# Four graph layers on one core: products of zeros at the start, two pairs fetched into idle places, later weights through GpSimd's queue

## The chip, the cores and the metric

The kernel runs on one core of a Trainium2 chip. The metric is the device time of one execution in microseconds. The kernel before was run three times: 521.82 us median, 519.45 to 524.5.

## The reference, cut to what matters

Four graph layers run one after the other on 3327 nodes of 64 features and one dense 3327 x 3327 adjacency matrix of floats. Each layer adds its result to its input and normalises each row.

```python
x = _layernorm(x + _L0_gnn_ref(x, adj, L0_gnn_W), axis=-1)
x = _layernorm(x + _L1_gnn_ref(x, adj, L1_gnn_weight, L1_gnn_bias), axis=-1)
x = _layernorm(x + _L2_gnn_ref(x, adj, L2_gnn_W, L2_gnn_b), axis=-1)
x = _layernorm(x + _L3_gnn_ref(x, adj, L3_gnn_weight, L3_gnn_bias), axis=-1)
```

The change is in layer 0, and in what layer 0 computes ahead for layer 3:

```python
# layer 0
neigh = jnp.matmul(adj, features)
deg = jnp.sum(adj, axis=1, keepdims=True) + 1.0
neigh = neigh / deg
data = jnp.concatenate([features, neigh], axis=-1)
return jnp.matmul(data, W.T)
# layer 3: only the last 100 neighbours of a node count
mask = (adj != 0).astype(support.dtype)
rank = jnp.cumsum(mask, axis=1)
```

## The kernel before, in words

**Tiling.** The nodes are padded to 26 blocks of 128. The adjacency matrix is stored transposed and read in four column chunks (CH = 832 nodes) by 13 pairs of row blocks: one pair is a tile of 128 x 2 x 832 floats, 832 KB. Every layer reads all 52 pairs again. In layer 0 the chunks go in the order 0, 3, 1, 2 (`ORDER`), and in each chunk the pairs go from jp = 12 down to jp = 0. `load_adj` (L307) issues a pair on SP's queue into the pool `adjp` of four buffers; a fifth load waits until the first buffer is free.

**Own features.** `load_xt` (L733) fetches the transposed features into `ut`, the first half of the tile `uw`: first the columns of the last blocks, and after three pairs the rest. `own_features` multiplies some blocks by the turned weights `w0r` (L686), into a bank of PSUM. ScalarE copies one half of the result to `x0w` (L692), the stationary operand of the aggregation, and VectorE copies the other to `xr` (L693). It is called at the pairs named in `heads`: jp 12, 11, 9, 6 and 2. The weights `w0` come on ScalarE's queue and are turned on VectorE (L177 to L188).

**One pair.** `aggregate_pair` (L482) adds the pair's product with `x0w` to the chunk's accumulator. For three of the four chunks the pair is also ranked for layer 3. VectorE makes a mask of nonzeros (L508). TensorE counts along it with triangular matrices (L554) in two banks, of the three that `own_features` also uses. ScalarE writes the ranks (L564), and VectorE carries the last row of the count into the mask of the next pair (L540). `count` is let behind: up to `L0_SPILL` = 6 masks are open at the end of the first chunk, and the second chunk, which isn't ranked, works them off.

**Order on each engine.** A scheduler places the instructions; `issue_after` gives it orderings. Each engine then works its queue in order. On VectorE the first three masks stand ahead of the first two `xr` copies, and the first count's bank is read by the first of those copies.

**Later weights.** At jp = 7 of the first chunk `load_weights` (L201 to L207) issues seven small loads on SP's queue, for layers 1 to 3. At jp = 2 `later_weights` turns them on VectorE (`turn` makes `w1h`) and sends two products through TensorE (L706, L707); the results go to `w1r`, `wl1` and `wl2` by copies of VectorE and ScalarE and memsets of GpSimd.

**The idle places.** `wt`, the second half of `uw`, is first written by `transposes0` in the second chunk. It holds two pairs. `half_of` gives one half of such a tile the shape of a pair; before, it stands further down, where layers 1 and 2 use it.

Of the kernel before, what the change touches and what calls it, by code (L numbers as in the profile page):

```python
# [21 lines left out]
BF = mybir.dt.bfloat16  # L22
# [10 lines left out]
P = 128  # L33
NB = 26
NP = NB * P
D = 64
CH = 832
HC = CH // 2
NCH = NP // CH

ORDER = (0, 3, 1, 2)
# [38 lines left out]

L0_SPILL = 6
L0_LAG = 3


L1_ENGINES = "GVGGGV"
# [42 lines left out]
def four_gnn_layers_kernel(  # L128
# [14 lines left out]
    nc = tc.nc  # L143
# [6 lines left out]
    setup = setup_stack.enter_context(tc.tile_pool(name="setup", bufs=1))  # L150
# [10 lines left out]
        out=basis, in_=basis, compare_op=ALU.not_equal, fill=55.0 / 56, base=0,  # L161
# [5 lines left out]
    def issue_after(ins, other):  # L167
        tc.add_manual_dep(
            ins.ins, other.ins.name,
            mybir.DependencyInfo(mybir.DependencyClass.NoSync, mybir.DependencyReason.DATA),  # L170
            reason="order",
        )
# [20 lines left out]
    w1s = setup.tile([D, D], FP, name="w1s")  # L193
    w2s = const.tile([D, 2, D], FP, name="w2s")
    w3s = const.tile([P, D], FP, name="w3s")
    b2s = const.tile([1, D], FP, name="b2s")
    bias = {name: const.tile([P, 1, D], FP, name=f"bias_{name}") for name in ("b1", "b3")}

    def load_weights():

        nc.sync.dma_start(out=w1s, in_=w1)  # L201
        nc.sync.dma_start(out=w2s, in_=w2.rearrange("(t k) f -> k t f", t=2))
        for h in range(2):
            nc.sync.dma_start(out=w3s[h * D : (h + 1) * D, :], in_=w3)
        nc.sync.dma_start(out=b2s, in_=b2.partition_broadcast(1))
        nc.sync.dma_start(out=bias["b1"][:, 0, :], in_=b1.partition_broadcast(P))
        nc.sync.dma_start(out=bias["b3"][:, 0, :], in_=b3.partition_broadcast(P))  # L207


    sign = const.tile([P, 1], FP, name="sign")  # L210
# [13 lines left out]
        out=tri, in_=tri, compare_op=ALU.is_gt, fill=0.0, base=0,  # L224
# [3 lines left out]
        out=tri, in_=tri, compare_op=ALU.not_equal, fill=float(MAX_NEIGH), base=0,  # L228
# [9 lines left out]
    for t, value in ((minus_last, -1.0), (last_bias, 200.0)):  # L238
        nc.gpsimd.memset(t, 0.0)
        nc.gpsimd.affine_select(  # L240
            out=t, in_=t, compare_op=ALU.not_equal, fill=value, base=1 - P,
# [11 lines left out]
        out=real, in_=real, compare_op=ALU.is_ge, fill=0.0, base=N - 1,  # L253
# [30 lines left out]
    ut, wt = uw[:, 0, :], uw[:, 1, :]  # L284
# [9 lines left out]
    last_rank = uw.rearrange("p t n -> p (t n)").bitcast(U8)[:, 0 : NB * CH]  # L294
    last_rank = last_rank.rearrange("p (b i) -> p b i", b=NB)


    def load_adj(c, jp, t=None):


        if isinstance(t, list):
            for k in range(2):
                nc.sync.dma_start(out=t[k], in_=adjt[c, 2 * jp + k])
            return t
        if t is None:
            t = adjp.tile([P, 2, CH], FP, name="adj", tag="adj")
        nc.sync.dma_start(out=t, in_=adjt[c, 2 * jp : 2 * jp + 2].rearrange("b p i -> p b i"))  # L307
        return t
# [236 lines left out]
    def count(masked, places, left=0, behind=None):  # L545

        issued = None
        while len(masked) > left:
            ranks, jp, mask, _ = masked.pop(0)
            counts = [places.zero(), places.one()]  # L550
            for k, lhsT, of in ((0, tri, 0), (1, tri, 1), (0, minus, 1)):
                for h in range(2):
                    for rows in (slice(0, D), slice(D, P)):
                        issued = nc.tensor.matmul(  # L554
                            counts[k][rows, h, 0:HC], lhsT=lhsT[:, rows],
                            rhs=mask[:, of, bass.ts(h, HC)],
                            start=lhsT is tri, stop=(k == 1 or lhsT is minus),
                        )
                        if behind is not None:
                            issue_after(issued, behind)  # L560
            ranks.after = counts[0]
            carry(masked)
            for k in (1, 0):
                ranks.made = nc.scalar.activation(  # L564
                    halves(ranks.rank[:, 2 * jp + k, :]), counts[k][:, :, 0:HC], AF.Relu,
                    bias=last_bias,
                )
        return issued
# [105 lines left out]
    with ExitStack() as l0s:  # L674
        banks = Banks(l0s, "l0psum")
        l0 = l0s.enter_context(tc.tile_pool(name="l0", bufs=1))
        mp = l0s.enter_context(tc.tile_pool(name="l0m", bufs=L0_SPILL + 3))
        places = Places(banks)
        x0w = l0.tile([P, NB, D], FP, name="x0w")
        nc.gpsimd.memset(x0w[:, :, 0:1], 1.0)  # L680

# [50 lines left out]
        def load_xt(cols):  # L732
            nc.sync.dma_start(out=ut[0:D, cols], in_=xt[:, cols])  # L733
# [2 lines left out]
        heads = {12: (24, 26), 11: (20, 24), 9: (13, 20), 6: (6, 13), 2: (0, 6)}  # L736
        first = GROUPS[3][0] * P
        load_xt(slice(first, NP))
        loaded = {jp: load_adj(ORDER[0], jp) for jp in (12, 11, 10)}
        load_xt(slice(0, first))  # L740
        masked, issued, counted, side = [], None, None, None
        for n, c in enumerate(ORDER):
# [4 lines left out]
            for jp in reversed(range(NB // 2)):  # L747
                owned = None
                if n == 0 and jp in heads:
                    owned = own_features(*heads[jp], issued if jp < 11 else None)  # L750
                a2 = loaded.pop(jp) if n == 0 and jp in loaded else load_adj(c, jp)
                issued = aggregate_pair(
                    acc, x0w, a2, jp, jp == NB // 2 - 1, jp == 0, counted or owned
                )
                if ranks:
                    mask = ranks.mask(jp, a2)
                    if n == 0:
                        issue_after(mask, turned)
                left = (L0_SPILL - jp // 2 if ranks else jp // 2) if n < 2 else L0_LAG
                counted = count(masked, places, left, issued)  # L760


                if side is not None and jp < NB // 2 - 1:
                    on_array = jp == NB // 2 - 2
                    if not step(side, (counted or issued) if on_array else mask if ranks else None):
                        side = None
                        transposes0(ORDER[n - 1], places.free(), counted or issued, True)
                        if n == NCH - 1:

                            nc.scalar.activation(nothing, wt[:, GROUPS[ORDER[n - 1]][0] * P].unsqueeze(1), AF.Tanh)  # L770
                if n == 0 and jp == 7:
                    load_weights()
                if n == 0 and jp == 2:
                    later_weights(mask)
# [412 lines left out]

    def half_of(t, k):
        return t[:, bass.ts(k, 2 * CH)].rearrange("p (b i) -> p b i", b=2)

    def load_ahead2(more):

        def load(k, t):
            return load_adj(ORDER2[0], PAIRS[k], t)

        loaded = [load(k, half_of(*t)) for k, t in enumerate(((ut, 0), (wt, 0), (wt, 1)))]
        yield loaded
        places = [[more(2 * i + k) for k in range(2)] for i in range(4)]
        loaded += [load(3 + k, t) for k, t in enumerate((*places, half_of(ut, 1)))]
        yield
        loaded.append(load(8, half_of(ut, 0)))
# [383 lines left out]
    with tc.If(some_near == 0) as cmp:  # L1590
        with ExitStack() as arm:
            banks = Banks(arm, "psum_far")
            layers_2_and_3(banks, *layer1_far(banks))
    with cmp.Else():
        done = layer1_near()
        with ExitStack() as arm:
            banks = Banks(arm, "psum_near")
# [47 lines left out]
```

## Time and profile before

| | |
|---|---|
| time, three runs | 521.82 us median, 519.45 to 524.5 |
| the profiled execution | 521.32 us, span 519.6 us |
| TensorE (PE) busy | 472.2 us, 91% |
| VectorE (DVE) busy | 392.6 us, 76% |
| ScalarE (ACT) busy | 341.2 us, 66% |
| GpSimd (POOL) busy | 205.9 us, 40% |
| moved by DMA | 132.49 MB, mean 255 GB/s |
| mean granted clock of TensorE | 0.986 |

Busy time is a share of the whole span; the stages differ. A line of the timeline gives start, duration, engine, source line, operation, tiles and count, and in brackets the idle time of the engine before it and what ended it. A line of the waits gives engine, tile and line, who was waited for, and then the total, the number and the longest of the waits. A line of the stretches gives the window, its length, busy time and instructions of PE, PE's weight loads, DVE, ACT and POOL, then PE's granted clock, the DMA share and GB/s. SPq is SP's DMA queue.

### The profile page before, as it was taken

How to read it: one execution, taken by the hardware profiler on the slowest of the kernel's cores; microseconds unless marked ns; L12 is line 12 of the kernel's file. 1: busy time of each engine (PE TensorE's matmuls, PEld its weight loads, DVE VectorE, ACT ScalarE, POOL GpSimd, SP SyncE). 2: the span in 40 equal slices, each digit the busy share in tenths (PEclk: the TensorE clock that was granted, in tenths of full speed). 3: DMA queues.
4: the chain of work that ended last, by engine and by line, in shares of the span. 5: the costliest groups of instructions: out<-in, count | busy, mean ns of one | idle time of the engine just before them, and what ended most of it. 6: DMA issues, size and time to landing. Idle time of an engine off the chain costs nothing. (4 is left out here: it accounts for less than half of the span.)

```text
span 519.6 us, 7871 instructions
## 1 busy us (share of the span) xinstructions
PE 472.2 (91%) x2888; PEld 241.7 (47%) x2888; DVE 392.6 (76%) x717; ACT 341.2 (66%) x422; POOL 205.9 (40%) x171
## 2 busy tenths in 40 slices
PE   5999999999967999999999999999999999899892
PEld 3554343454433333443353344354465555467781
DVE  3566428989767987789879977988789487737894
ACT  1345544776877899968987796820278845579862
POOL 2000200203017778966896785700412053410650
PEclk9999999999998999999999999999999999999995
DMA  8899999989529678767776777579969889960002
GB/s 271 280 387 322 390 376 368 356 289 328 199 69 308 241 264 280 245 198 256 252 245 202 236 259 261 197 275 401 316 195 360 305 289 345 316 240 2 0 2 71
DMA packets 46289, 132.49 MB, mean 255 GB/s; under 512 B 7046, under 2 KB 7150, under 8 KB 46178
## 3 DMA queue, kind: packets, MB, share of 16 engines
q1 hardware_dynamic: 45714, 131.36, 72.4%
q0 software_dynamic: 384, 0.52, 0.4%
q8 instruction: 24, 0.39, 0.3%
q14 instruction: 23, 0.19, 0.1%
q10 hardware_dynamic: 144, 0.03, 0.0%
HBM read 130.88 MB, written 0.85 MB: 254 GB/s over the span
## 5 line engine op out<-in xcount | busy, mean ns | idle before, releaser
L878 POOL TENSOR_TENSOR s<-s,p 128x832 f32<-128x832 f32 x67 | 130.2, 1957 | 43.5 <-ACT s L877 27.9
L863 DVE SCALAR_TENSOR_TENSOR p<-two,adj 128x832 f32<-128x832 f32 x100 | 101.1, 1018 | 19.7 <-issue 12.9
L564 ACT ACTIVATE rank<-two,last_bias 128x832 uint8<-128x832 f32 x78 | 71.7, 953 | 46.4 <-PE two L554 24.5
L852 PE MATMUL two<-uw 64*128 64x416 f32 x416 | 89.7, 545 | 13.1 <-DVE s L871 6.0
L482 PE MATMUL one<-adj,x0w 128*64 128x416 f32 x416 | 83.0, 524 | 3.8 <-DMA adj<-in_adjt_dram 2.4
L883 PE MATMUL one<-s,xu 128*64 128x416 f32 x416 | 85.2, 524 | 0.0
L540 DVE SCALAR_TENSOR_TENSOR mask<-two,minus_last,mask 32x832 bf16<-32x832 f32 x48 | 52.5, 1093 | 32.8 <-PE two L554 28.7
L876 ACT ACTIVATE s<-two 128x832 f32<-128x832 f32 x67 | 57.7, 861 | 28.8 <-DVE p L863 25.6
L852 PEld LDWEIGHTS two<-uw 64*128 64x128 f32 x416 | 38.2, 189 | 64.6 <-PE one L883 20.7
L508 DVE TENSOR_SCALAR mask<-adj 128x1664 bf16<-128x1664 f32 x48 | 51.3, 1070 | 14.0 <-DMA adj<-in_adjt_dram 13.5
L877 ACT ACTIVATE s<-s 128x832 f32<-128x832 f32 x67 | 60.1, 897 | 1.9
L554 PE MATMUL two<-mask,tri 128*64 128x416 bf16 x416 | 53.3, 345 | 8.5 <-DVE mask L540 5.4
L482 PE MATMUL one<-adj,xr 128*64 128x416 f32 x264 | 53.7, 517 | 2.4 <-DMA adj<-in_adjt_dram 2.4
L883 PEld LDWEIGHTS one<-s,xu 128*64 128x64 f32 x416 | 25.8, 136 | 47.5 <-issue 46.7
L482 PEld LDWEIGHTS one<-adj,x0w 128*64 128x64 f32 x416 | 29.0, 138 | 36.8 <-issue 23.6
L554 PEld LDWEIGHTS <-tri 128*64 128x64 bf16 x416 | 26.2, 110 | 40.9 <-issue 24.3
L1375 ACT ACTIVATE bits<-rank 128x832 fp32r<-128x832 uint8 (+1 forms) x42 | 38.8, 987 | 6.9 <-PE two L1430 5.1
L1371 POOL TENSOR_SCALAR bits<-exponents 128x832 fp32r<-128x832 bf16 (+1 forms) x21 | 26.0, 1255 | 40.5 <-DVE exponents L1353 20.4
L871 DVE SCALAR_TENSOR_TENSOR s<-two,p 128x832 f32<-128x832 f32 x37 | 37.5, 1015 | 1.4 <-ACT two L868 1.3
L868 ACT ACTIVATE two<-two 128x832 f32<-128x832 f32 x37 | 31.3, 847 | 5.4 <-DVE p L863 4.6
L1430 PE MATMUL two<-bits,parts 128*128 128x416 f32 x144 | 30.9, 360 | 2.5 <-POOL bits L1371 2.4
L482 PEld LDWEIGHTS one<-adj,xr 128*64 128x64 f32 x264 | 21.0, 136 | 23.2 <-issue 16.5
(290 smaller groups left out, 542.4 us busy)
## 6 DMA issues: line engine op xcount, KB each, us to landing
adj<-in_adjt_dram SPq DMA_DIRECT2D x135, 832.0 KB, 5.5
uw<-in_adjt_dram SPq DMA_DIRECT2D x7, 832.0 KB, 6.2
a<-in_adjt_dram SPq DMA_DIRECT2D x8, 416.0 KB, 6.5
sums<-in_adjt_dram SPq DMA_DIRECT2D x2, 832.0 KB, 7.4
p<-in_adjt_dram SPq DMA_DIRECT2D x4, 416.0 KB, 4.9
s<-in_adjt_dram SPq DMA_DIRECT2D x4, 416.0 KB, 6.5
uw<-in_xt_dram SPq DMA_DIRECT2D x1, 640.0 KB
out_dram<-o SPq DMA_DIRECT2D x2, 192.0 KB, 2.3
```

The lines of the kernel that those rows point to most:

```text
L482: issued = nc.tensor.matmul(acc[h * D : (h + 1) * D, 0:HC], lhsT=x[:, 2 * jp + k, 0:D], rhs=a[:, bass.ts(h, HC)], start=(first and k == 1) ...
L508: issued = nc.vector.tensor_scalar(mask, a2, 0.0, None, op0=ALU.not_equal)
L540: ranks.carried = nc.vector.scalar_tensor_tensor(halves(last), ranks.after[P - 32 : P, :, 0:HC], minus_last[P - 32 : P, :], halves(last), ...
L554: issued = nc.tensor.matmul(counts[k][rows, h, 0:HC], lhsT=lhsT[:, rows], rhs=mask[:, of, bass.ts(h, HC)], start=lhsT is tri, stop=(k == 1 ...
L564: ranks.made = nc.scalar.activation(halves(ranks.rank[:, 2 * jp + k, :]), counts[k][:, :, 0:HC], AF.Relu, bias=last_bias,)
L852: issued = nc.tensor.matmul(v[:, h, 0:HC], lhsT=wt[rows, bass.ts(jb, P)], rhs=ut[rows, bass.ds(c * CH + h * HC, HC)], start=True, stop=True,)
L863: issued = nc.vector.scalar_tensor_tensor(halves(p), v, 0.25 - 0.5 * FD, halves(a), op0=ALU.add, op1=ALU.mult)
L876: nc.scalar.activation(halves(s), v, AF.Square, bias=FB - 0.5, scale=-2.0)
L877: nc.scalar.activation(s, s, AF.Copy, bias=FG)
L878: nc.gpsimd.tensor_mul(s, s, p)
L883: issued = nc.tensor.matmul(acc[h * D : (h + 1) * D, 0:HC], lhsT=xu[:, jb, 0:D], rhs=s[:, bass.ts(h, HC)], start=first, stop=last,)
L1375: issued = nc.scalar.activation(t, src[:, b, :], AF.Exp, bias=-127.0 * LN2, scale=LN2)
```

## The change

A tile of zeros is cleared by VectorE, and thirteen bf16 products of it (`L0_IDLE`) go through TensorE into a bank that the counts use later, ahead of the first own features. The first two pairs of the first chunk (jp 12 and 11) go into the two halves of `wt`; the third goes into the pool, whose four buffers then take jp 10, 9, 8 and 7. The seven loads of `load_weights` move from SP's queue to GpSimd's, where they stand behind the memset of `x0w`. `half_of` is defined further up.

```diff
+L0_IDLE = 13
...
     def load_weights():
-        nc.sync.dma_start(out=w1s, in_=w1)
-        nc.sync.dma_start(out=w2s, in_=w2.rearrange("(t k) f -> k t f", t=2))
+        nc.gpsimd.dma_start(out=w1s, in_=w1)
+        nc.gpsimd.dma_start(out=w2s, in_=w2.rearrange("(t k) f -> k t f", t=2))
         for h in range(2):
-            nc.sync.dma_start(out=w3s[h * D : (h + 1) * D, :], in_=w3)
-        nc.sync.dma_start(out=b2s, in_=b2.partition_broadcast(1))
-        nc.sync.dma_start(out=bias["b1"][:, 0, :], in_=b1.partition_broadcast(P))
-        nc.sync.dma_start(out=bias["b3"][:, 0, :], in_=b3.partition_broadcast(P))
+            nc.gpsimd.dma_start(out=w3s[h * D : (h + 1) * D, :], in_=w3)
+        nc.gpsimd.dma_start(out=b2s, in_=b2.partition_broadcast(1))
+        nc.gpsimd.dma_start(out=bias["b1"][:, 0, :], in_=b1.partition_broadcast(P))
+        nc.gpsimd.dma_start(out=bias["b3"][:, 0, :], in_=b3.partition_broadcast(P))
...
+    def half_of(t, k):
+        return t[:, bass.ts(k, 2 * CH)].rearrange("p (b i) -> p b i", b=2)
...
         places = Places(banks)
+        zeros = setup.tile([P, HC], BF, name="zeros")
+        nc.vector.memset(zeros, 0.0)
+        idle = banks.pair(1)
+        for _ in range(L0_IDLE):
+            nc.tensor.matmul(
+                idle[:, 0, 0:HC], lhsT=zeros[:, 0:P], rhs=zeros, start=True, stop=True
+            )
...
         load_xt(slice(first, NP))
-        loaded = {jp: load_adj(ORDER[0], jp) for jp in (12, 11, 10)}
+        loaded = {
+            jp: load_adj(ORDER[0], jp, half_of(wt, 12 - jp) if jp > 10 else None)
+            for jp in (12, 11, 10)
+        }
         load_xt(slice(0, first))
```

The scheduler's order changes with it in a few places of the first chunk. On TensorE the two products of `later_weights` stand right behind the last own features and ahead of pair 2's aggregation, where before they stood behind the count that follows that aggregation. On VectorE the turning of the later weights moves ahead of the last `xr` copy, and the mask of pair 6 and that of pair 2 move ahead of a carry. On ScalarE the two copies into `wl1` and `wl2` move ahead of and between two rank writes. Behind the first steps of the second chunk the order on every engine is as before.

## The prediction

> **What bounds the kernel now.** I read the page's slices first (where the transfers pause), then busy time by stretches, then the waits, then the timeline of the first 45 us, because every edit acts there. Pairs of adjacency blocks are called by their jp: 12 comes first, 0 last.
>
> The stretches (length, busy us and instructions of each engine, clock, DMA share, GB/s):
>
> ```profile
> 20.00:22.00 2.00, 1.16 (x9) 0.53 (x10) 1.62 (x3) 0.80 (x2) 0.00 (x0) 1.00 0.24 45
> 24.00:41.00 17.00, 16.44 (x126) 9.09 (x120) 11.94 (x26) 7.35 (x9) 0.00 (x0) 1.00 1.00 372
> 41.00:48.00 7.00, 7.00 (x48) 3.20 (x48) 3.85 (x8) 4.60 (x8) 0.78 (x5) 1.00 0.86 261
> 48.00:60.00 12.00, 11.47 (x84) 4.86 (x80) 7.44 (x25) 6.80 (x9) 3.16 (x4) 1.00 1.02 391
> 60.00:76.00 16.00, 14.42 (x100) 6.78 (x98) 3.21 (x3) 8.98 (x11) 0.29 (x1) 1.00 1.02 388
> ```
>
> TensorE is full until 48 us, while the transfers have a hole at 20 to 22 us (45 GB/s) and are thin at 41 to 48 us (261 GB/s). From 48 to 76 us, the second chunk, the transfers are full (391 GB/s) and TensorE has holes. So the first chunk is paced by TensorE and the second by the transfers. The waits say the same:
>
> ```profile
> PE two L554 <- DVE xr L693: 0.7, 1, 0.7
> ...
> SPq L307 <- PE one L482: 77.3, 46, 4.3
> ```
>
> Between 12 and 45 us no TensorE matmul waits for a pair of the adjacency; SP's queue waits for TensorE to release one of four buffers. The start itself:
>
> ```profile
> 8.64 3.04 PE L482 MATMUL one<-adj,x0w 128*64 128x416 f32 x8
> ...
> 11.09 1.03 DVE L508 TENSOR_SCALAR mask<-adj 128x1664 bf16<-128x1664 f32 x1 [1.60 <-DMA adj<-in_adjt_dram]
> 12.03 0.61 DVE L693 COPY xr<-two 128x126 f32<-128x126 f32 x2
> 12.37 1.60 PE L554 MATMUL two<-mask,tri 128*64 128x416 bf16 x8 [0.68 <-DVE xr L693]
> ...
> 16.26 0.47 SPq L201 DMA_DIRECT2D w1s<-in_w_dram  x1
> ...
> 20.91 19.13 SPq L307 DMA_DIRECT2D adj<-in_adjt_dram  x9
> ...
> 24.75 1.57 PE L482 MATMUL one<-adj,x0w 128*64 128x416 f32 x8
> ```
>
> The same eight products take 3.04 us at 8.64 and 1.57 us at 24.75: TensorE starts at half clock. The clock record of the trace begins at full speed at 14.03 us. But the chain at the start isn't TensorE's. The first count (L554, 12.37) wants a bank that the xr copy (L693) reads; that copy stands on VectorE behind the mask of pair 10, the third pair, which landed at 11.09. That order on VectorE (three masks, then the copies) is the same in the changed program.
>
> **The change part by part.** The sum starts from the profiled execution, 521.32 us (span 519.6, 1.7 around it). The median of the three runs is 521.82, their spread 519.45 to 524.5.
>
> *Thirteen products of zeros.* VectorE clears the tile ahead of its first work at 4.44 us, by a memset like GpSimd's 0.2 us ones. A bf16 product of 416 columns takes 0.35 us at half clock (the L554 pairs at 12.37), so 13 x 0.35 = 4.55 us, from about 1.1 to 5.7 us. First operands come at 5.79: on the path 0 to +0.2 us, and I take 0, since the next wait (12.37) covers it. If the clock is then full, twelve feature products (2.93 us) and eight aggregations (3.04 us) take 1.5 each and end near 8.9 instead of 11.68. The gain is a longer wait for the same xr copy: 0.
>
> *What the clock does in that wait.* TensorE would be idle from 8.9 to 12.4, 3.5 us. What idleness did later in this trace:
>
> ```profile
> 157.39:160.80 3.41, 1.21 (x6) 0.30 (x4) 3.41 (x5) 3.23 (x4) 1.67 (x4) 1.00 1.06 377
> 160.80:164.21 3.41, 3.32 (x10) 1.90 (x12) 1.40 (x3) 2.58 (x4) 3.41 (x3) 0.50 1.04 268
> ...
> 505.55:508.96 3.41, 1.83 (x15) 1.55 (x13) 2.26 (x8) 1.08 (x2) 0.00 (x0) 1.00 0.48 118
> ```
>
> The record changes at 14.03, 160.80, 164.21 and 508.96, all whole multiples of 3.413 us apart. A stretch of that length with TensorE busy 1.21 us (36%) was followed by half clock, and so was one at 1.83 us (54%); 2.01 and 2.12 us (59 and 62%) were not. However the grid lies, a hole of 3.5 us leaves one stretch under 50%, so by the nearest rows the clock falls again and rises only after a well-filled stretch, somewhere from 14.3 to 18.6 us, against 14.03 now. Ends: if it stays full, the first count takes 1.05 instead of 1.85 us and the rank, the carry (L540) and the second count (17.02) follow 0.7 us earlier: -0.7. If it is half until 18.6, the aggregations of pairs 11 and 10 (2.8 us at full clock) take up to 2.3 us more: +2.3. For half clock until 15.7, the middle of the grid, it is +0.9. I weigh falling twice as heavy as staying: +0.4.
>
> [...]
>
> *Pairs 12 and 11 into idle places.* Now the fifth and sixth pairs (8 and 7) are issued at 11.72 and 15.84, each on a release by TensorE. In the changed program they go out at once behind pair 9. SP then issues pair 6 near 17, when pair 10 is released, and no longer at 20.91. From pair 5 on every issue waits for the same TensorE release as before (22.51 now, behind the aggregation that ended at 22.25). Nothing on TensorE waited for pairs 9 to 0, so their earlier landing hides nothing: 0. If the transfers were the bound, closing the hole would bring 2.0 x (391 - 45)/391 = 1.8 us; that is the far end.
>
> *Weights on GpSimd's queue.* Seven issues leave SP, where they held it from 16.26 to 20.1; that is the lateness of pair 6 above, counted already. GpSimd issues loads at 0.51 to 0.73 us each (155 to 158 us), so from about 4 to 8 us; three memsets queued behind them (L715 to L717) are wanted only in layer 1. Their 577 packets of 256 B at 18 ns are 0.68 us of the 16 engines. They now fall into full transfers, partly ahead of pair 10, whose landing sets 12.37: 0 to +0.7, taken +0.2.
>
> *What the scheduler moves.* The two products of later_weights (L706, L707) now stand right behind the last own features and ahead of pair 2. There TensorE waits for ScalarE today:
>
> ```profile
> 38.02 1.62 PE L482 MATMUL one<-adj,x0w 128*64 128x416 f32 x8 [0.56 <-ACT x0w L692]
> ...
> 40.62 0.33 PE L706 MATMUL two<-w1h,basis 64*64 64x64 f32 x2
> ```
>
> They cost 0.47 us at 40.62 (to 41.09) and would fill that wait: -0.45. But they need w1h, which VectorE makes 1.04 us after starting (38.46 to 39.50), now behind the mask of pair 2 and a carry (1.09). If mask 2 starts at 34.4, w1h is there at 37.5 and TensorE, free at 37.45, loses nothing. Mask 2 started at 35.69; if it does again, w1h comes at 38.8 and everything behind L706 is 1.2 us late. Ends -0.45 and +1.2; taken -0.45, since pair 2's transfer has less queued ahead of it. The carry for pair 0 moves behind the mask of pair 0 on VectorE, to about 42.7, still ahead of its count (43.98 now): 0.
>
> Sum: 0 + 0.4 + 0 + 0.2 - 0.45 = +0.15, so 521.5 us. A shift at the end of the first chunk goes on whole: the second is a closed loop of transfers that begins with releases by TensorE, and what follows has TensorE or VectorE over 85% busy (76 to 100 us: 22.98 and 20.55 of 24).
>
> **The rivals.**
>
> *Transfers set the first 48 us.* For it: both thin stretches, and eight TensorE waits for pairs, 6.5 us, from 45 to 80 us. Then the hole gives 1.8 us, the thin stretch 7 x (391 - 261)/391 = 2.3, the clock 0.7 and the moved products 0.45: 5.25, so 516.1 us. Against it: no TensorE wait for a pair between 12 and 45 us, and four buffers as before from pair 5 on, so the thin stretch stays.
>
> *The clock falls in the new hole and stays down until 18.6 us.* It decides from a rise later than 14.5 us on. Price +2.3 in place of +0.4: 523.4 us, slower than before. For it: the 36% and 54% stretches. Against: it needs an unlucky grid.
>
> *L706 waits for w1h at the head of TensorE's queue.* It decides if mask 2 starts later than 34.4 us; price 1.65 against the sum: 523.2. For it: mask 2 at 35.69 now. Against: pair 6 is issued 3 to 4 us earlier.
>
> *The zeros don't do what they are for:* the clock rises at 14 us as now. Then the 0.4 goes: 521.1.
>
> **How the numbers follow.** Forecast 0.50, transfers 0.12, clock down 0.18, w1h 0.12, idle zeros 0.08. The forecast is 521.5, no change. About 1% (5.2 us) is what a measurement of this kernel can tell from no change. The term bounds give 520.2 (-0.7 - 0.45) to 525.7 (0.2 + 2.3 + 0.7 + 1.2). The spread of the runs and part of the transfer case widen the lower side, and the top is cut where all bad ends would have to meet: 517.3 to 524.6. Faster by over 1% (under 516.6) is half the transfer case and a little scatter: 0.07. Slower by over 1% (over 527.0) needs two bad ends together: 0.05. Within: 0.88.
>
> **What would show it.** Right: L554's first count still at 12.3 to 12.8 behind the xr copy; L482's first eight in under 2.2 us; a half-clock stretch or 0.70 us steps of L482 again after 12 us; pair 6 issued near 17; the last aggregation of the first chunk ending within 2 us of 45; waits for pairs in the second chunk as now. Wrong: the second count (17.02) or the second chunk starting over 2.5 us earlier, the thin stretch at 41 to 48 us gone, or any difference made behind 80 us.

## The result, and the profile after

The changed kernel takes 527.33 us (median of 6 runs, 525.88 to 530.19) against 521.5 us for the kernel before in the same session (6 runs, 519.45 to 524.5). The ratio is 1.0119, 95% interval 1.0086 to 1.0152: 5.8 us slower, above the upper end of the forecast's range. The ratios, here and below, come from fast runs alone and are not quotients of two medians, from which they can differ by up to half a per cent. The profiled execution took 527.99 us, its span is 526.3 us (519.6 before), the mean granted clock 0.976 (0.986 before). Most lines of the changed kernel stand 6 to 13 further down: L482 is now L488, L508 L514, L540 L546, L554 L560, L564 L570, L692 and L693 are L705 and L706, L706 and L707 are L719 and L720, L597 is L603. The products of zeros are L689. In the other kernels the numbers shift again by a few lines.

The same stretches as before the change, with the hole of the transfers, which moved, in a stretch of its own (length, busy us and instructions of PE, PEld, DVE, ACT and POOL, clock, DMA share, GB/s):

```profile
20.00:22.00 2.00, 1.39 (x13) 1.20 (x11) 1.80 (x2) 1.47 (x3) 0.00 (x0) 1.00 1.03 388
22.00:24.00 2.00, 1.77 (x10) 0.77 (x12) 1.55 (x2) 0.17 (x1) 0.00 (x0) 1.00 0.30 112
24.00:41.00 17.00, 14.83 (x110) 8.23 (x106) 9.90 (x19) 6.16 (x8) 0.00 (x0) 0.97 0.90 312
41.00:48.00 7.00, 6.67 (x30) 3.02 (x32) 4.58 (x15) 1.82 (x5) 1.69 (x5) 0.58 0.47 152
48.00:60.00 12.00, 12.00 (x92) 5.81 (x90) 4.33 (x13) 7.39 (x9) 0.99 (x1) 1.00 0.97 339
```

The hole at 20 us is filled (45 GB/s before, 388 now) and another stands at 22 us (112 GB/s, and 83 from 24 to 26 us). The new thing is in the third and fourth rows. From 24 to 41 us TensorE did 110 instructions where it did 126, and from 41 to 48 us the clock is 0.58 where it was 1.00. By 48 us the second chunk, which used to begin at 45.03, has not begun. The timeline puts its first transposes 5.7 us later, of the 6.7 us by which the span is longer (before, then after):

```profile
49.09 0.58 PE L597 MATMUL one<-ident,sums 64*128 64x64 f32 x6
```

```profile
54.76 0.58 PE L603 MATMUL one<-ident,sums 64*128 64x64 f32 x6
```

The waits from 12 to 48 us (total, times, longest):

```profile
DVE mask L514 <- DMA adj<-in_adjt_dram: 8.2, 5, 2.5
...
ACT rank L570 <- DVE mask L546: 6.4, 4, 3.6
...
PE two L560 <- DVE xr L706: 4.0, 1, 4.0
...
PE two L719 <- DVE turn_m L186: 2.5, 1, 2.5
```

TensorE has two long waits: 4.0 us for the xr copy, which was 0.7 us before, and 2.5 us at the head of its queue, in L719, the first later-weight product, where before no wait in that place exceeded 0.6 us. The timeline at the first:

```profile
1.21 4.69 PE L689 MATMUL two<-zeros 128*128 128x416 bf16 x13 [1.21 <-DVE zeros L686]
5.89 1.60 PE L699 MATMUL two<-w0r,uw 64*128 64x128 f32 x12
7.43 1.62 PE L488 MATMUL one<-uw,x0w 128*64 128x416 f32 x8
...
13.01 1.60 PE L560 MATMUL two<-mask,tri 128*64 128x416 bf16 x8 [3.96 <-DVE xr L706]
```

The zeros do what they are for: the twelve own features take 1.60 us (2.93 before) and the first eight aggregations 1.62 (3.04). They end at 9.04 us, and TensorE then idles until 13.01, because the xr copy still stands on VectorE behind the mask of pair 10:

```profile
11.73 1.03 DVE L514 TENSOR_SCALAR mask<-adj 128x1664 bf16<-128x1664 f32 x1 [2.17 <-DMA adj<-in_adjt_dram]
```

That mask began at 11.09 before; it is 0.64 us later. At the second wait, before and after:

```profile
34.56 1.09 DVE L540 SCALAR_TENSOR_TENSOR mask<-two,minus_last,mask 32x832 bf16<-32x832 f32 x1 [0.18 <-PE two L554]
35.69 1.03 DVE L508 TENSOR_SCALAR mask<-adj 128x1664 bf16<-128x1664 f32 x1
...
37.49 0.47 ACT L692 COPY x0w<-two 128x378 f32<-128x378 f32 x1 [0.84 <-PE two L686]
```

```profile
37.23 1.60 PE L699 MATMUL two<-w0r,uw 64*128 64x128 f32 x12
...
37.95 1.03 DVE L514 TENSOR_SCALAR mask<-adj 128x1664 bf16<-128x1664 f32 x1 [2.45 <-DMA adj<-in_adjt_dram]
39.01 1.09 DVE L546 SCALAR_TENSOR_TENSOR mask<-two,minus_last,mask 32x832 bf16<-32x832 f32 x1
...
40.14 0.95 ACT L570 ACTIVATE rank<-two,last_bias 128x832 uint8<-128x832 f32 x1 [3.60 <-DVE mask L546]
...
40.94 0.24 DVE L187 TENSOR_SCALAR w1h<-w1s,turn_m 64x63 f32<-64x63 f32 x1
40.99 0.47 ACT L705 COPY x0w<-two 128x378 f32<-128x378 f32 x1
...
41.33 0.44 PE L719 MATMUL two<-w1h,basis 64*64 64x64 f32 x2 [2.50 <-DVE turn_m L186]
```

VectorE waits 2.45 us for pair 2 to land, then makes its mask, then the carry (L546; before, the carry came first, at 34.56 us), then what leads to w1h. On ScalarE the rank waits 3.60 us for that carry, and the x0w copy for pair 2 stands behind the rank. So two things that TensorE needs next, w1h and x0w, are both late by a wait for a transfer that neither of them reads.

Pair 2 is late for two reasons. SP issues it when TensorE releases its buffer, and that came 1.4 us later than before (29.66 us before, then 31.04), about as much as TensorE had lost at the start (the second count came at 18.39 us, before at 17.02). And the transfer itself took 6.9 us from issue to landing where it had taken 5.8; over the 19 profiles it took 4.7 to 6.9 us.

```profile
29.66 0.37 SPq L307 DMA_DIRECT2D adj<-in_adjt_dram  x1
```

```profile
31.04 0.37 SPq L313 DMA_DIRECT2D adj<-in_adjt_dram  x1
```

Both waits cost twice. These are the stretches around them of the grid on which the clock's record changes (at 5.92, 12.75, 16.16, 40.06 and 46.88 us in this profile, all whole multiples of 3.413 us apart):

```profile
9.34:12.75 3.41, 0.00 (x0) 0.00 (x0) 1.24 (x3) 0.00 (x0) 0.44 (x3) 1.00 1.12 290
12.75:16.16 3.41, 3.16 (x16) 1.96 (x17) 0.53 (x3) 1.46 (x2) 0.00 (x0) 0.50 0.94 288
...
36.64:40.06 3.41, 2.19 (x16) 1.41 (x12) 2.07 (x2) 0.00 (x0) 0.00 (x0) 1.00 1.02 367
40.06:43.47 3.41, 2.14 (x8) 1.02 (x10) 3.35 (x21) 1.36 (x3) 0.02 (x1) 0.50 0.76 303
43.47:46.88 3.41, 3.41 (x18) 1.53 (x16) 1.31 (x3) 0.45 (x2) 1.53 (x4) 0.50 0.21 21
```

After each wait TensorE runs at half clock: 12.75 to 16.16, and 40.06 to 46.88 us, where the aggregation of pair 2 takes 3.04 us in place of 1.62.

### The profile page after: what moved, and what is told of

The parts are those of the page before. It is cut to its first block, busy times and chain, and to the rows that moved or that the text cites. A ratio compares the mean times of both kernels' runs of the same rounds, so it can differ in the third digit from the quotient of the medians.

```text
span 526.3 us, 7899 instructions
## 1 busy us (share of the span) xinstructions
PE 477.7 (91%) x2901; PEld 243.3 (46%) x2901; DVE 392.6 (75%) x718; ACT 341.1 (65%) x422; POOL 212.5 (40%) x178
## 5 line engine op out<-in xcount | busy, mean ns | idle before, releaser
L570 ACT ACTIVATE rank<-two,last_bias 128x832 uint8<-128x832 f32 x78 | 71.7, 953 | 52.1 <-PE two L560 26.0
L488 PE MATMUL one<-adj,x0w 128*64 128x416 f32 x400 | 79.6, 524 | 3.1 <-DMA adj<-in_adjt_dram 2.2
L546 DVE SCALAR_TENSOR_TENSOR mask<-two,minus_last,mask 32x832 bf16<-32x832 f32 x48 | 52.5, 1093 | 33.9 <-PE two L560 29.6
L560 PE MATMUL two<-mask,tri 128*64 128x416 bf16 x416 | 53.9, 350 | 11.8 <-DVE mask L546 5.4
L514 DVE TENSOR_SCALAR mask<-adj 128x1664 bf16<-128x1664 f32 x46 | 48.6, 1057 | 18.9 <-DMA adj<-in_adjt_dram 18.4
L488 PE MATMUL one<-adj,xr 128*64 128x416 f32 x264 | 54.0, 517 | 2.2 <-DMA adj<-in_adjt_dram 2.2
L560 PEld LDWEIGHTS <-tri 128*64 128x64 bf16 x416 | 26.3, 111 | 44.2 <-issue 27.9
L488 PEld LDWEIGHTS one<-adj,x0w 128*64 128x64 f32 x400 | 28.1, 139 | 35.0 <-issue 23.6
L488 PEld LDWEIGHTS one<-adj,xr 128*64 128x64 f32 x264 | 20.9, 136 | 23.3 <-issue 16.1
```

Source lines behind the costliest of these rows:

```text
L488: issued = nc.tensor.matmul(acc[h * D : (h + 1) * D, 0:HC], lhsT=x[:, 2 * jp + k, 0:D], rhs=a[:, bass.ts(h, HC)], start=(first and k == 1) ...
L514: issued = nc.vector.tensor_scalar(mask, a2, 0.0, None, op0=ALU.not_equal)
L546: ranks.carried = nc.vector.scalar_tensor_tensor(halves(last), ranks.after[P - 32 : P, :, 0:HC], minus_last[P - 32 : P, :], halves(last), ...
L560: issued = nc.tensor.matmul(counts[k][rows, h, 0:HC], lhsT=lhsT[:, rows], rhs=mask[:, of, bass.ts(h, HC)], start=lhsT is tri, stop=(k == 1 ...
L570: ranks.made = nc.scalar.activation(halves(ranks.rank[:, 2 * jp + k, :]), counts[k][:, :, 0:HC], AF.Relu, bias=last_bias,)
```

## The experiments

The theory from these lines: most of the loss is the scheduler's new order. Rivals: the zeros (with the hole behind them), the weights' packets ahead of pair 10, and the two pairs. Each ratio is against the kernel before, run on the same chip beside it, where its median stood between 520.8 and 522.1 us.

**1. What of the change loses the time.** The first four kernels undo one part or do one part alone.

*e1_pin*: the changed kernel with the two later-weight products held behind the count of pair 2 on TensorE.

```diff
-            nc.tensor.matmul(tp[0:D, 0, 0:D], lhsT=basis, rhs=w1h, start=True, stop=True)
+            one = nc.tensor.matmul(tp[0:D, 0, 0:D], lhsT=basis, rhs=w1h, start=True, stop=True)
+            issue_after(one, counted)
```

> The changed kernel, with the two products of later_weights held behind the count of pair 2, where the kernel before has them. Theory W (the products wait for w1h at the head of TensorE's queue, and the clock falls in that wait): the wait of 2.5 us at 38.83 and the half-clock stretch from 40.06 to 46.88 go, the 1.4 us lost by the second count stay: 522 to 523.5 us. Theory S (the start of the kernel loses the time, and the rest only follows): 526.5 to 528. Theory E (the loss lies elsewhere, behind the first chunk): 526.5 to 528, with the wait gone from the trace.

Measured: 527.42 us, ratio 1.0088 (1.0060 to 1.0117). The wait has only changed its name:

```profile
37.91 1.09 DVE L546 SCALAR_TENSOR_TENSOR mask<-two,minus_last,mask 32x832 bf16<-32x832 f32 x1
...
39.04 0.95 ACT L570 ACTIVATE rank<-two,last_bias 128x832 uint8<-128x832 f32 x1 [2.76 <-DVE mask L546]
...
40.41 0.96 PE L488 MATMUL one<-adj,x0w 128*64 128x416 f32 x2 [1.84 <-ACT x0w L705]
```

With the products out of the way TensorE waits for the x0w copy, and the clock falls from 39.78 to 43.20. The products at the head of the queue, the rival that the prediction had named, are not the cause by themselves.

*e2_weights_on_sp*: the changed kernel with the loads of the weights back on SP's queue (zeros and pairs stay).

> The changed kernel with the seven later weights back on SP's queue; zeros and the two pairs in idle places stay, and the order of all engines is that of the kernel before. Theory W: the order on TensorE came with the queue, so the wait goes with it, and so do the weights' packets ahead of pair 10 (0.6 us); what is left is the clock in the hole at 9 to 12.4 us, -0.7 to +1.0: 520.5 to 522.5 us. Theory S with the zeros as its cause: 525 to 528. Theory P (the pairs in idle places take away transfers that hid something): 525 to 528.

Measured: 523.15 us, 1.0021 (0.9989 to 1.0052). Without the loads on GpSimd's queue the order on every engine is that of before, and the loss can no longer be told from nothing. Its profiled execution was unlike the others from the start: the first pair landed at 7.44 us (6.16 to 6.59 in all others) and pair 10 at 13.19, so that one profile is a poor measure of this kernel.

*e3_no_zeros*: the changed kernel without L686 to L689.

> The changed kernel without the thirteen products of zeros; the order on all engines is otherwise the changed one. Theory W: the wait for w1h stays and the clock falls in it again; the first fall at 12.75 can't come: 525 to 527 us. Theory S with the zeros as its cause: 520.5 to 522.5.

Measured: 528.67 us, 1.0091 (1.0052 to 1.0129). Most of the loss stays, and the time is above what either theory had told; TensorE waits from 36.99 to 39.52, and the clock falls from 38.62 to 45.45.

*e4_only_pool*: the kernel before with the weights on GpSimd's queue and nothing else.

> The kernel before with one part of the change alone, the seven later weights on GpSimd's queue. The two products stand ahead of pair 2 here as well. Theory W: pair 2 lands no earlier than with all parts, so the wait for w1h is there: 524 to 527 us. Theory S with the zeros, or theory P, as the cause: 520.5 to 522.5.

Measured: 525.6 us, 1.0058 (1.0025 to 1.0091). Its profiled execution was a quick one, 521.9 us: the wait is there (37.42 to 39.39 us), but the clock didn't fall in it.

**2. The scheduler's order.** *e5_all_old_order* has all parts of the change, with the first chunk's order on VectorE, ScalarE and TensorE held as in the kernel before; *e6_no_zeros_old_order* is the same without zeros; *e11_queue_alone_old_order* has the queue alone.

```diff
                     if n == 0:
                         issue_after(mask, turned)
+                        if jp in (6, 4, 2, 0):
+                            issue_after(mask, ranks.carried)
+                        if jp in (7, 5, 1):
+                            issue_after(mask, copied[0])
...
-                    later_weights(mask)
+                    later_weights(copied[0], counted)
```

> All parts of the change, with VectorE's, ScalarE's and TensorE's order in the first chunk held as the kernel before has it. e1 moved the two products back and stayed slow: in its trace TensorE waits 1.84 us at 38.57 for the x0w copy, which stands behind a rank, which waits for the carry (L546), which stands behind the mask of pair 2, which waits for its pair. Theory O (that order on VectorE, which came with the move of the loads to GpSimd's queue, is the loss): 521.5 to 523.5 us, the rest being the clock in the hole at 9 to 13 us and the weights' packets. Theory Q (the loads on GpSimd's queue cost by themselves, by their packets or their landing): 526 to 528.

> As e5, without the zeros. Theory O: the clock rises at 11 to 14 us and doesn't fall again, 521 to 522.5 us, at most 1.5 below e5. If the zeros pay by themselves: 1 us or more above e5.

> The kernel before with the later weights on GpSimd's queue alone, and the order of masks, carries and products in the first chunk held as before. Theory A (the queue costs only through the scheduler's order): ratio 0.998 to 1.002, and not 1.006 as with the scheduler's own order. Theory B (577 packets ahead of pair 10 delay its mask and all behind it): ratio 1.003 to 1.006, and the mask of pair 10 starts 0.5 us or more later than 11.09.

Measured: e5 524.08 us, 1.0052 (1.0027 to 1.0077); e6 523.63 us, 1.0050 (1.0019 to 1.0081); e11 522.84 us, 1.0003 (0.9966 to 1.0040). Each stands 0.4 to 0.7% under its twin with the scheduler's order: 1.0119 against 1.0052, 1.0091 (e3) against 1.0050, 1.0058 (e4) against 1.0003; only in the first of these do the intervals lie apart. In all three the wait at 38 us is the 0.56 us of before again. e5 and e6 still lie above what theory O had told (523.5 and 522.5 us at most). In e11 the packets are still early and pair 10 still late:

```profile
11.61 1.03 DVE L514 TENSOR_SCALAR mask<-adj 128x1664 bf16<-128x1664 f32 x1 [1.93 <-DMA adj<-in_adjt_dram]
...
12.89 0.89 PE L560 MATMUL two<-mask,tri 128*64 128x416 bf16 x8 [1.23 <-DVE xr L701]
```

The first count is 0.5 us later than before (12.37), and no clock is lost.

**3. Which link of that order.** *e13_masks_first* puts into the kernel before only the exchange seen on VectorE (`issue_after(ranks.carried, mask)` at pairs 6 and 2). *e17_copy_ahead_of_rank* is e1 with the x0w copy ahead of the waiting rank on ScalarE (`issue_after(ranks.made, wide[0])`, where `wide[0]` is that copy).

> The kernel before, with two neighbours exchanged twice on VectorE in the first chunk: the masks of pairs 6 and 2 stand ahead of a carry, as in the changed kernel; no load is moved. Theory A (the order alone makes the wait): TensorE waits 1 to 2.5 us near 38 us for the x0w copy behind the rank behind the carry behind the mask of pair 2; ratio 1.002 to 1.006. Theory B (the order costs only when pair 2 also lands later, as it does with the weights on GpSimd's queue): pair 2 is there at 34.4, the carry comes 1 us later than now, the wait at 38 grows from 0.56 to about 1.5 us; ratio 1.0 to 1.002.

> The changed kernel with the two later weight products behind the count of pair 2, as in e1, and one exchange on ScalarE: the x0w copy of the last own features stands ahead of the rank that waits for the late carry. VectorE keeps the scheduler's order (mask of pair 2 ahead of the carry). Theory A (the copy behind the rank is the link): the wait near 38 us is 0.6 us as before, no half clock from 40 us on, ratio 1.003 to 1.006 where e1 had 1.0088 (what is left is zeros and early packets). Theory B (the late mask and carry hold the count anyway): the wait only moves to the count behind pair 2's aggregation, ratio 1.007 to 1.010.

Measured: e13 522.3 us, 1.0024 (0.9984 to 1.0064): not told from nothing. Its timeline (all engines) shows why it is no full copy of the changed order:

```profile
36.31 1.09 DVE L540 SCALAR_TENSOR_TENSOR mask<-two,minus_last,mask 32x832 bf16<-32x832 f32 x1
36.48 0.47 ACT L692 COPY x0w<-two 128x378 f32<-128x378 f32 x1 [2.32 <-PE two L686]
37.01 1.62 PE L482 MATMUL one<-adj,x0w 128*64 128x416 f32 x8 [0.56 <-ACT x0w L692]
37.44 0.55 DVE L693 COPY xr<-two 128x378 f32<-128x378 f32 x1
37.44 0.95 ACT L564 ACTIVATE rank<-two,last_bias 128x832 uint8<-128x832 f32 x1 [0.48 <-DVE mask L540]
```

The scheduler put the x0w copy ahead of the rank, and the xr copy directly behind the carry. The late carry then hurts nobody. e17 made only the first of these exchanges: 527.18 us, 1.0129 (1.0097 to 1.0162), above what either theory had told.

```profile
39.61 1.62 PE L488 MATMUL one<-adj,x0w 128*64 128x416 f32 x8 [0.56 <-ACT x0w L707]
...
42.91 0.89 PE L560 MATMUL two<-mask,tri 128*64 128x416 bf16 x8 [1.68 <-DVE mean L746]
```

The wait for x0w is 0.56 us as before, and the count behind it waits 1.68 us. In the changed order the last xr copy, which frees a bank, stands behind the carry, the work for w1h and the mask of pair 1 (on VectorE at 41.27 in this run). The copy ended at 42.86 us; the profile names the tiny L746 just behind it, so that the bank ended this wait is read from the order and not shown. So three things queue behind the mask of pair 2 on VectorE: w1h, x0w by way of the rank, and the bank. Taking away one showed the next (e1, e17); with the whole line in its old order the wait was away (e5, e6, e11). (The clock didn't fall in this profile's 1.68 us, yet the median is no better than that of the changed kernel.)

**4. The remaining half per cent.** With the old order 0.5% remains. Two kernels do one part alone, *e9_zeros_alone* and *e10_pairs_alone*. *e14_queue_and_zeros_old_order* leaves out the pairs. *e15_late_queue_and_pairs* and *e16_all_late_queue* (with zeros) hold the loads on GpSimd behind a small copy that reads the first xr copy (`read` is `xr[:, NB - 1, 1:2]`), so that their packets come behind pair 10:

```diff
+        first = nc.gpsimd.tensor_copy(late, read)
...
+        for load in loads:
+            issue_after(load, first)
```

> The kernel before with the thirteen products of zeros and nothing else. Theory A (the zeros gain nothing, because they only move the wait in front of the xr copy): the first aggregations run at full clock and end near 9 us, TensorE then waits about 3.5 us for the xr copy, the clock may fall after that, the first chunk ends within 1.5 us of before (41.1 us); time 520 to 524, ratio 0.997 to 1.005. Theory B (the fall of the clock in that hole is the rest of 0.5% that the versions with the old order still lose): ratio 1.004 to 1.008, and the half-clock stretch ends after 14.5 us.

> The kernel before with the two pairs fetched into the idle places and nothing else; the order on every engine is that of before. Theory A (nothing waited for these pairs, so earlier landing hides nothing): 520.5 to 522.5, ratio 0.998 to 1.003, first chunk ends at 41 us as before, the hole in the transfers closes or moves. Theory B (transfers that start earlier crowd pair 10 and later ones): ratio 1.003 to 1.006.

> The kernel before with the weights on GpSimd's queue and the thirteen products of zeros, order of the first chunk held as before, no pairs fetched ahead. Theory A (the remaining 0.5% belongs to pairs ahead together with the queue): ratio 0.998 to 1.003. Theory B (the later pair 10 and the clock's fall in the hole before the xr copy add up: hole 9 to 13 us, half clock until 16 to 18 us): ratio 1.003 to 1.007, second chunk starts 1 us or more later than 45.03.

> The kernel before with the two pairs fetched ahead and the weights on GpSimd's queue, but their loads held behind a small copy on GpSimd that reads the first xr copy (near 12 us), no zeros, order of the first chunk held as before. Theory A (the weights' packets ahead of pair 10 make the remaining loss): mask of pair 10 near 11.1 as before, ratio 0.997 to 1.002. Theory B (the remaining loss has to do with the pairs ahead, whatever the packets): ratio 1.003 to 1.006.

> All three parts of the change, order of the first chunk held as before, the weights' loads on GpSimd held behind the first xr copy. Theory A (the rest of 0.5% is the weights' packets ahead of pair 10): ratio 0.998 to 1.002, mask of pair 10 at 11.1 to 11.3. Theory B (the rest is the zeros: the clock falls or does not rise in the hole that they leave): ratio 1.003 to 1.007, with half clock somewhere between 9 and 18 us, whatever the mask of pair 10 does. Halfway, as zeros alone were measured (1.0024), would leave both.

Measured, and beside it the start of the first transposes of the second chunk (one profile each; 49.09 us before):

| | zeros | pairs | early packets | time, us | ratio | transposes, us |
|---|---|---|---|---|---|---|
| e9 | yes | | | 523.13 | 1.0024 (0.9989 to 1.0058) | 50.15 |
| e10 | | yes | | 522.34 | 0.9996 (0.9964 to 1.0028) | 48.65 |
| e11 | | | yes | 522.84 | 1.0003 (0.9966 to 1.0040) | 48.73 |
| e14 | yes | | yes | 525.89 | 1.0064 (1.0031 to 1.0098) | 50.88 |
| e15 | | yes | | 521.37 | 0.9997 (0.9967 to 1.0028) | 48.35 |
| e16 | yes | yes | | 524.91 | 1.0044 (1.0012 to 1.0076) | 49.86 |
| e2 | yes | yes | | 523.15 | 1.0021 (0.9989 to 1.0052) | 52.99 |
| e6 | | yes | yes | 523.63 | 1.0050 (1.0019 to 1.0081) | 49.01 |
| e5 | yes | yes | yes | 524.08 | 1.0052 (1.0027 to 1.0077) | 51.36 |

Every kernel with the zeros is 1.0 to 2.4 us later at the transposes than its twin without them (e9 and before, e14 and e11, e16 and e15, e5 and e6); e2 is 4.3 us behind e10, in the profile that began late. The timeline of TensorE in e16 shows how:

```profile
12.33 0.96 PE L566 MATMUL two<-mask,tri 128*64 128x416 bf16 x8 [3.11 <-DVE xr L714]
13.04 0.96 PE L566 MATMUL two<-mask,minus 128*64 128x416 bf16 x4
13.73 2.94 PE L494 MATMUL one<-uw,x0w 128*64 128x416 f32 x8
16.47 1.59 PE L494 MATMUL one<-adj,x0w 128*64 128x416 f32 x8
```

The first count begins at 12.33 us, as before the change (12.37). But the clock, raised at 6.20, is half again from 13.03 to 16.44 us, and eight aggregations take 2.94 us in place of some 1.6. In e14's profile the zeros failed in the other way:

```profile
1.21 4.69 PE L689 MATMUL two<-zeros 128*128 128x416 bf16 x13 [1.21 <-DVE zeros L686]
5.93 2.93 PE L701 MATMUL two<-w0r,uw 64*128 64x128 f32 x12
8.79 3.04 PE L488 MATMUL one<-adj,x0w 128*64 128x416 f32 x8
```

The products of zeros ran, and the clock stayed at half until 17.36 us. The grid lay so that its stretches were 0.30 to 3.71 and 3.71 to 7.12 us. Zeros held 2.50 us of the first and 2.19 us of the second, whose rest the own features filled. In the eight other profiles with zeros the stretch that ended in the rise held 2.65 us of them or more. The stretch from 7.12 to 10.54 us was busy throughout with features and aggregations and did not raise the clock either; why is open.

A sum over all of it: I fitted the ratios of twelve kernels (the changed one, e2 to e6, e9 to e11, e14 to e16) by one addend for each part, weighted by their intervals. It gives zeros +0.28% (plus or minus 0.17), pairs +0.06% (0.15), early packets +0.26% (0.18), the scheduler's order +0.49% (0.25). The four add up to 1.09%, against 1.19% measured, and no kernel is off by more than 0.23%. Several kernels share the same runs of before, so these intervals are rough. In us of 521.5: 1.5, 0.3, 1.3 and 2.6. So the order is the largest part but, against the theory at the start, not most of the loss. The fit takes for granted that the parts add up. Pairs alone and early packets alone lose nothing (e10, e11), and together 0.5% (e6); whether they act on each other or this is scatter is open.

**5. A way around the xr copy.** Since that copy waits behind the mask of pair 10, three kernels put that mask behind the first carry: in e5 (*e7_xr_first*), in e6 (*e8_xr_first_no_zeros*), and in the kernel before alone (*e12_first_copy_sooner*).

```diff
-                        if jp in (6, 4, 2, 0):
+                        if jp in (10, 6, 4, 2, 0):
```

> As e5, and the mask of pair 10 stands behind the first xr copies and the first carry on VectorE, so that the first count doesn't wait for pair 10. Theory H (the zeros gained nothing because that wait took it all, and the clock fell in it): the hole at 9 to 13 us shrinks below 1 us, the clock stays up, the second count comes 3 us earlier; TensorE then waits for pair 9 and the rest of the features at 14 to 17 us: 518 to 520 us. If the start hides behind the transfers whatever TensorE does: as e5.

> As e7, without the zeros. TensorE is at half clock until 11 to 14 us, so the first count can start only at 11.7 instead of 9: theory H says 1 to 2 us above e7, 519.5 to 521.5 us. If the zeros have no worth even without the wait: as e7.

> The kernel before with one order changed on VectorE: the mask of pair 10 stands behind the xr copy and the first carry, so that the first count no longer waits for pair 10 to land. Weights on SP, no zeros, no pairs ahead. If that copy was what set the start, the first count begins near 11.7 (end of the first aggregations) in place of 12.37, and the first chunk ends up to 0.7 us sooner: 520.5 to 521.5, ratio 0.997 to 1.0. If the mask of pair 10, now later, holds the counts behind it, the gain is lost there: ratio 1.0 to 1.003.

Measured: e7 523.79 us, 1.0045 (1.0015 to 1.0074); e8 523.4 us, 1.0018 (0.9990 to 1.0047); e12 521.65 us, 1.0001 (0.9969 to 1.0034). In e7 the first count begins at 9.68 us and the second at 13.53, 3.5 us sooner than before the change, as theory H had told. But TensorE then waits 3.75 us for an x0w copy and the clock falls (17.71 to 24.54 us), so the forecasts of 518 to 520 us for e7 and 519.5 to 521.5 us for e8 failed. In e12 the first count begins at 11.35 us, 1.0 us sooner, and the gain is handed back further on (timeline, two engines):

```profile
19.21 0.95 ACT L570 ACTIVATE rank<-two,last_bias 128x832 uint8<-128x832 f32 x1 [1.24 <-DVE mask L546]
20.06 0.52 ACT L700 COPY x0w<-two 128x441 f32<-128x441 f32 x1
...
20.63 1.62 PE L488 MATMUL one<-adj,x0w 128*64 128x416 f32 x8 [1.55 <-ACT x0w L700]
```

It is the same chain as at 38 us: a carry behind a mask, a rank behind the carry, an x0w copy behind the rank. Before, the aggregation behind it started at 20.85 us. No kernel tried is measurably faster than the kernel before.

## Why the prediction was wrong, point by point

**The zeros: 0 us.** Right as told: features at full clock, ended at 9.04 (8.9 told), and the gain became a longer wait for the xr copy.

**The clock in that wait: +0.4 us.** The fall came as told and the size was too small. The clock fell again in each of the profiles with zeros that keep the copy where it was (at 12.75 us in the changed kernel, 11.29 in e5, 13.22 in e9, 13.03 in e16), except in e14, where it had not risen. The fit puts the zeros' whole effect at 1.5 us (0.9 either way), inside the told ends (-0.7 and +2.3), where +0.9 had been worked out for a fall and weighed down. The author's estimate was that a stretch of the grid less than half busy is followed by half clock. In the changed kernel's profile the stretch from 9.34 to 12.75 us was wholly idle and fits it; the one from 36.64 to 40.06 was busy for 2.19 us of 3.41 and was also followed by half clock.

**The two pairs: 0 us.** Right: e10 at 0.9996, and +0.06% in the fit. But the hole in the transfers did not close as told. In e10 it stays (69 GB/s from 20 to 22 us), and in the changed kernel it moved to 22 to 26 us: pair 6 went out at 18.61 us and pair 5 only at 23.89, each released by TensorE. Nor did closing it pay: in e15 the hole is nearly gone (371 GB/s from 20 to 22 us, 235 from 22 to 24), and the ratio is 0.9997. That speaks against the rival "transfers set the first 48 us", as does that in the changed kernel, too, no TensorE product waits for a pair between 12 and 45 us.

**The weights' packets: +0.2 us.** Pair 10's mask came 0.64 us later, as the far end (+0.7) had it. The delay is steady: in the nine profiles with early loads where that mask waits for its pair it starts at 11.41 to 11.90 us, in the six with late loads at 10.88 to 11.24 (e2 left out). The loss in time is not: the fit says 1.3 us, with 0.9 us either way, and e11 alone shows none. That the packets cost time is likely and not shown.

**What the scheduler moves: -0.45 us.** This is the step that failed. It took the mask of pair 2 to start at 34.4 us, with less queued ahead of its transfer; it started at 37.95. The prediction itself had said that from pair 5 on every issue waits for TensorE: pair 2 went out 1.4 us later than before, with TensorE's later release, and its transfer took 1.1 us longer, not less. It priced only w1h behind it, at +1.2 us at worst. It missed that the rank, the x0w copy and the xr copy hang on the same line of VectorE, as e1 and e17 show, and that a wait there can be followed by half clock a second time (40.06 to 46.88 after a wait of 2.50 us; after 1.84 in e1, and not after 1.97 in e4's profile). The order's cost by the fit is 2.6 us (1.3 either way), where a gain of 0.45 had been told.

The rival "L706 waits for w1h at the head of TensorE's queue" named the place and too small a price (1.65 us), and as a mechanism it is only a part of the story, since with these products out of the way e1 still lost 0.9%. "The clock falls in the new hole" came true beside it. The range's top had been cut because both bad ends "would have to meet". They met: the early loads delay pair 10, and moving them is what changed the order, so these ends were no independent draws.

## What to carry to other kernels

When an edit makes a scheduler move one instruction that waits for a transfer ahead of others, list everything behind it on that engine and everything that waits for those, on every engine; cost the line, not its first victim. A faster start in front of a fixed wait is not free where half clock follows the wait, as it did here from 12.75 to 16.16 us after a wait of 3.96 us: price the clock after the wait too. And terms that come from one cause should not be treated as independent when a range is cut.

## What the runs showed of the hardware

The clock's record didn't follow the busy share of TensorE in the stretch of the grid before. In the changed kernel half clock followed stretches with 0.00 and 2.19 us busy of 3.41 (0 and 64%), in e3 one with 1.78 (52%), and in e2 one that was busy throughout (the first line); the products of L488 behind it came every 0.69 us, and every 0.35 once the clock had risen. In e17 a stretch with 1.73 us (51%) and in e9 one with 1.58 us (46%) were followed by full clock:

```profile
347.51:350.92 3.41, 3.41 (x30) 3.27 (x28) 1.92 (x5) 1.00 (x2) 0.00 (x0) 1.00 0.95 328
```

```profile
40.79:44.20 3.41, 1.73 (x18) 0.84 (x15) 3.30 (x11) 0.36 (x1) 0.00 (x0) 1.00 0.96 340
```

```profile
453.54:456.95 3.41, 1.58 (x8) 0.45 (x8) 0.89 (x2) 1.31 (x2) 0.93 (x1) 1.00 0.95 338
```

Over the 19 profiles, every stretch at full clock with less than 1.58 us busy (24 of them) was followed by half clock. Above that both happen, so the prediction's line between 54 and 59% does not hold. The 25 falls behind a stretch with 1.75 us busy or more have one thing in common: ten or more of the products that start in it are fp32 ones that move only 64 to 128 columns, as the own features do, and at most four move 416. Whether that decides the fall was not tested, and what decides it stays open.

The grid of 3.413 us lies anew in each execution (the first rise of the clock came at 14.03 us before, 12.40 in e10, 13.16 in e12 and 11.23 in e11). Between 145 and 170 us the kernel before lost one stretch to half clock, e10 and e12 two, and e11 none, which then had the shortest span of all profiles (517.4 us). That the grid's place decides it fits these rows and is not shown; it would be one source of the spread of several us between executions of one kernel (519.45 to 524.5 us before).
